# Portioning softmax work between matrix products, and giving the products' PSUM banks a pool of their own, in a two-layer cross-attention kernel

## The chip, the cores and the metric

The kernel runs on one core of one Trainium2 chip. The metric is the time of one execution on the device in microseconds (us), as the median of several runs. The core's engines work side by side and meet by semaphores: PE does the matrix products and transposes and writes its results into PSUM, which has eight banks; DVE (vectors), ACT (activations, copies) empty them; POOL does some elementwise work and issues the stores; SP issues the loads.

## The reference

Two layers of cross-attention over the same context, for B = 8 batch items of S = 100 tokens with C = 640 channels and 20 heads of 32. The context has 722 rows of 1024: the first 77 are text, the other 645 are image rows.

```python
# layer 0
q = split(x @ Wq.T);  k, v = split(text @ Wk.T), split(text @ Wv.T)
k_ip, v_ip = split(ip @ Wk_ip.T), split(ip @ Wv_ip.T)
out = attend(q, k, v) + attend(q, k_ip, v_ip)          # softmax(q k / sqrt(32)) v, each
x = out @ Wo.T + bo + x
# layer 1: the same with weights not transposed, and
text_probs = softmax(q_all @ k_text_all.T / sqrt(32))  # over all 640 channels
sem = (text_probs @ text) @ ip.T / sqrt(32)
ip_probs = softmax(scores_ip + 0.5 * sem) * spatial_mask
x = (text_out + ip_probs @ v_ip) @ Wout + bout + x
```

All of it is in fp32. Text and image have a softmax each.

## The kernel before

**Prologue.** Inside a `with` block the queries of layer 0 and the keys and values of the text rows of both layers are made and stored to device memory. Products of two blocks by two blocks are done with seven block products in place of eight (`seven`, lines 158 to 205): first, sixth, second, seventh, fifth, fourth, third. The second and the third add to the bank that the first and the fifth have opened; before they may, ACT has copied the first out (L172), and DVE has combined the fifth with another block (L192). The others are emptied by ACT (L181) or DVE (L177 to L203). The functions of the prologue are `text_k`, `text_v`, `text_v_blocks`, `left_v`, `left_text`, and `sums_of`, which makes the weights' sums (L131 to L134). Every product takes its bank from `product_ps`, which asks the pool `pj[0]`; in the prologue that is `ps_first`, with all eight banks. After the block the pools `ps_sc` (one tile of four banks for scores), `ps_pt` (two banks, for transposes and small products) and `ps_pj` (two banks, for products) take their place.

**Main loop.** A unit u is one batch item of one layer (16 in all), and in it p runs over five groups of four heads; n = 5u + p counts the 80 steps. In a step the kernel does the attention of group (u, p) and, in between, produces keys and values of the image rows for later units. Production is a list of tasks, each one product or a part of one of about 2 us, with a due time in steps (`spread`, from rough costs). `make(until)` runs the tasks whose due time has come; `between` puts them around small products (output projection `out_piece`, next queries `q_piece`, and the four functions `sem_...` for layer 1). The tasks are those of `pair_tasks` (two batch items at a time with `seven`: psv and psk; `last_k` makes the fifth block of keys, L503, copied by ACT at L509), then `single_tasks` and `last_tasks` (plain products, L608, copied at L610).

The order in a step is: scores part 0 (512 image rows); products; transposes 0 and 1 of the step before; products; transposes 2 and 3; scores part 1 (133 image rows and 77 text rows); products; transposes 4 and 5; products; `values` of the step before (pv, L927). After each pair of transposes, DVE (L912) or ACT (L910, blocks 2 and 5) copies the transposed block out.

`scores` (line 840) multiplies queries with keys into the tile sc (L849) and then asks for the whole softmax of that part at once: the negated maxima (one DVE reduce over four heads for layer 0, L855; for layer 1 one DVE operation a head, L862, that also adds sem), an exponential a head (ACT, L866), and for part 1 the text maxima (L872), the text exponentials (L874), the factors that join the two parts (L879 to L887), and the scaling of the probabilities p (four ACT operations L889, two DVE operations L890 and L893).

**What sets the order.** The loop is in a `manual_schedule` for PE: PE runs exactly in the order of the code. The instructions of the other engines are put in order by the framework ahead of the run, and on the chip each engine follows that fixed order.

Of the kernel before, what the change touches and what calls it, by code (L numbers as in the profile page):

```python
# [10 lines left out]
AF = mybir.ActivationFunctionType  # L11
ALU = mybir.AluOpType
AX = mybir.AxisListType
# [3 lines left out]
S = 100  # L17
C = 640
CC = 1024
NT = 77  # L20
NI = 645
NL = NI - 5 * P
NK = NI + NT
KA = 512
KB = NK - KA
# [18 lines left out]
def two_layer_xattn(  # L44
# [17 lines left out]
    nc = tc.nc  # L62
    PSUM = bass.MemoryType.PSUM
# [22 lines left out]
    mask_sb = const.tile([S, 2], F32, tag="mask", name="mask_sb")  # L86
# [52 lines left out]
    def load_wk(src):  # L139
        load_quarters("k", src, 2 * P)  # L140
        W["k", 4] = wpool.tile([P, NCC, P], F32, tag="wk4", name="wk4")
        nc.sync.dma_start(W["k", 4], src.rearrange("(k p) n -> p k n", p=P)[:, :, 4 * P :])
# [7 lines left out]

    def product_ps(name):
        return pj[0].tile([P, 512], F32, tag="pj", name=name)

    pj = []

    def seven(name, product, area, beside=None):

# [59 lines left out]
    TR = TH - 2 * P  # L219
    with ExitStack() as es:  # L220
        fp = es.enter_context(tc.tile_pool(name="first", bufs=1))
        pj.append(es.enter_context(tc.tile_pool(name="ps_first", bufs=8, space=PSUM)))
        xt = fp.tile([P, B, NC_, S], F32, tag="x", name="xt")
        wq0 = []
        nc.sync.dma_start(xt[:, :2], x_t[:, :2])
# [6 lines left out]
        text = fp.tile([P, NCC, B * NT], F32, tag="text", name="text")  # L232
# [12 lines left out]
        for g in range(B // 2):  # L245
# [10 lines left out]
            for i in range(3):  # L256
                n = 2 if i < 2 else 1
# [7 lines left out]
        st = fp.tile([P, 4, HK, TH], F32, tag="s", name="s_text")  # L265
# [53 lines left out]
                    t[64 * h : 64 * h + TR, :, :HC],  # L319
                )  # L320

        def text_v_blocks(l, rows=(0, 1)):
            for r in rows:
                t = fp.tile([P, 2, 2, HC], F32, tag="evs", name=f"vt_{l}_{r}", bufs=2)

                def product(ps, which, go_on, r=r):
                    for k in range(HK):
                        nc.tensor.matmul(
                            ps[:, :HC], lhsT=sums[which][:, k, r * P : (r + 1) * P], rhs=W["v", WHICH[which]][:, k, :],
                            start=(k == 0 and not go_on), stop=(k == HK - 1), skip_group_check=True,  # L330
                        )

                for f in seven(f"psvt_{l}_{r}", product, tuple(t[:, h, m] for h in range(2) for m in range(2))):
                    f()
                for h in range(2):
                    nc.gpsimd.dma_start(
                        vt_d[l][h * TH + r * P : h * TH + (r + 1) * P, :].rearrange("r (m n) -> r m n", m=2), t[:, h]
                    )
# [3 lines left out]
        def load_left(l):  # L342
            for k in range(NCC):
                wl[l, k] = fp.tile([P, C], F32, tag="wr", name=f"wl_{l}_{k}", bufs=NCC)
                nc.sync.dma_start(wl[l, k], wvi[l][k * P : (k + 1) * P, :])
# [37 lines left out]
        def sums_of(kind):  # L383
            weight_sums(kind, {"v": HC, "k": 2 * P}[kind], (nc.vector, nc.gpsimd))

        with tc.manual_schedule(engines={mybir.EngineType.PE}):
            sums_of("k")
            text_k(0)
            load_wk(wkt[1])
            text_v(0)  # L390
            sums_of("v")
            load_left(0)
            text_v_blocks(0)
            load_wv(wvt[1])
            sums_of("k")
            text_k(1)
            load_wk(wki[0])
            left_v(0)
            load_left(1)
            left_text()  # L400
            text_v(1)
            sums_of("v")
            text_v_blocks(1, (0,))
            sums_of("k")
            left_v(1)
            text_v_blocks(1, (1,))

    ps_sc = ctx.enter_context(tc.tile_pool(name="ps_sc", bufs=1, space=PSUM))
    ps_pt = ctx.enter_context(tc.tile_pool(name="ps_pt", bufs=2, space=PSUM))
    pj[0] = ctx.enter_context(tc.tile_pool(name="ps_pj", bufs=2, space=PSUM))  # L410
    opool = ctx.enter_context(tc.tile_pool(name="made", bufs=2))
    kpool = ctx.enter_context(tc.tile_pool(name="k", bufs=2))
    vpool = ctx.enter_context(tc.tile_pool(name="v", bufs=2))
# [5 lines left out]
    ks, vs, qs_, vts, sems, texts, kt5 = {}, {}, {}, {}, {}, {}, {}  # L419
# [417 lines left out]

    pr, stats, sct = {}, {}, {}

    def scores(u, c, part):  # L840
        k0, k1 = ((0, KA), (KA, NK))[part]
        if part == 0:
            pr[u, c] = ppool.tile([S, 4, NK], F32, tag="p", name=f"p_{u}_{c}")

            stats[u, c] = stat.tile([S, 14, 4], F32, tag="st", name=f"st_{u}_{c}")
        sc = ps_sc.tile([P, 4, 512], F32, tag="sc", name=f"sc_{u}_{c}_{part}")
        for i in range(4):
            rows = slice(32 * i, 32 * i + 32)
            nc.tensor.matmul(  # L849
                sc[:S, i, : k1 - k0], lhsT=qs_[u][rows, c, :], rhs=ks[u, c][rows, k0:k1], start=True, stop=True  # L850
            )
        p, st, l = pr[u, c], stats[u, c], u // B
        n = min(k1, NI) - k0
        if l == 0:
            nc.vector.tensor_reduce(st[:, part, :], sc[:S, :, :n], AX.X, ALU.max, negate=True)  # L855
        for i in range(4):
            if l == 0:
                img, sign = sc[:S, i, :n], 1.0
            else:

                img, sign = p[:, i, k0 : k0 + n], -1.0
                nc.vector.tensor_tensor_reduce(  # L862
                    out=img, in0=sc[:S, i, :n], in1=sems[u][:, k0 : k0 + n], scale=-1.0, scalar=3.0e38,
                    op0=ALU.add, op1=ALU.min, accum_out=st[:, part, i : i + 1],
                )
            nc.scalar.activation(  # L866
                p[:, i, k0 : k0 + n], img, AF.Exp, bias=st[:, part, i : i + 1], scale=sign,
                accum_out=st[:, 3 + part, i : i + 1],
            )
        if part == 0:  # L870
            return
        nc.vector.tensor_reduce(st[:, 2, :], sc[:S, :, n:KB], AX.X, ALU.max, negate=True)  # L872
        for i in range(4):
            nc.scalar.activation(  # L874
                p[:, i, NI:], sc[:S, i, n:KB], AF.Exp, bias=st[:, 2, i : i + 1], accum_out=st[:, 5, i : i + 1]
            )

        lo, f, rz, mul = st[:, 6, :], st[:, 7:9, :], st[:, 9:11, :], st[:, 11:13, :]
        nc.vector.tensor_tensor(lo, st[:, 0, :], st[:, 1, :], ALU.min)  # L879
        nc.vector.tensor_tensor(f, lo.unsqueeze(1).to_broadcast([S, 2, 4]), st[:, 0:2, :], ALU.subtract)  # L880
        nc.scalar.activation(f, f, AF.Exp)
        nc.vector.tensor_tensor(st[:, 3:5, :], st[:, 3:5, :], f, ALU.mult)
        nc.vector.tensor_tensor(st[:, 4, :], st[:, 3, :], st[:, 4, :], ALU.add)
        nc.vector.reciprocal(rz, st[:, 4:6, :])
        nc.vector.scalar_tensor_tensor(  # L885
            mul, f, mask_sb[:, l : l + 1], rz[:, 0:1, :].to_broadcast([S, 2, 4]), ALU.mult, ALU.mult
        )  # L887
        for i in range(4):
            nc.scalar.activation(p[:, i, :KA], p[:, i, :KA], AF.Copy, scale=mul[:, 0, i : i + 1])  # L889
        nc.vector.tensor_tensor(  # L890
            p[:, :, KA:NI], p[:, :, KA:NI], mul[:, 1, :].unsqueeze(2).to_broadcast([S, 4, NI - KA]), ALU.mult
        )
        nc.vector.tensor_tensor(  # L893
            p[:, :, NI:], p[:, :, NI:], rz[:, 1, :].unsqueeze(2).to_broadcast([S, 4, NT]), ALU.mult
        )

    pts = {}

    def transposes(u, c, j):
        if j == 0:  # L900
            pts[u, c] = one.tile([P, 6, 4 * S], F32, tag="pt", name=f"pt_{u}_{c}")
        rows = P if j < 5 else NTAIL
        ps = ps_pt.tile([P, 512], F32, tag="pt", name=f"pspt_{u}_{c}_{j}")
        for i in range(4):
            nc.tensor.transpose(  # L905
                ps[:rows, i * S : (i + 1) * S], pr[u, c][:, i, j * P : j * P + rows], ident[:S, :S]
            )
        dst, src = pts[u, c][:rows, j, :], ps[:rows, : 4 * S]
        if j % 3 == 2:
            nc.scalar.copy(dst, src)  # L910
        else:
            nc.vector.tensor_copy(dst, src)  # L912
# [126 lines left out]
    with tc.manual_schedule(engines={mybir.EngineType.PE}):  # L1039
# [5 lines left out]
        todo = production()  # L1045
        done = [0]

        def make(until):
            while done[0] < len(todo) and todo[done[0]][1] < until:
                todo[done[0]][2]()  # L1050
                done[0] += 1

        mark = [0]

        def apart(until):

            while done[0] < len(todo) and todo[done[0]][1] < until and not any(
                t for t, _, _ in todo[mark[0] : done[0]]
            ):
                todo[done[0]][2]()  # L1060
                done[0] += 1
            mark[0] = done[0]

        def between(n, a, b, small):
# [11 lines left out]
        for u in range(NU):  # L1076
            for p in range(NC_):
                n = NC_ * u + p
# [78 lines left out]
```

## Time and profile before

| what | value |
|---|---|
| median of 3 runs | 2101.18 us (2100.68 to 2103.62) |
| the profiled execution's own time | 2102.57 us |
| its span, first to last instruction | 2100.8 us |
| granted clock of PE | 1.000 |
| prologue, up to the first product of the loop | 207.6 us |
| first scores | 396 us |

The span is 1.8 us shorter than the execution's own time. Rows of groups read: line, engine, operation, output <- input, shapes, count | busy us, mean ns of one | idle time of the engine just before them, and what ended it. In the timeline a row begins with its start and its duration; a bracket gives the idle time of its engine just before it and what released it.

### The profile page before, as it was taken

The page shows a single profiled execution, that of the slowest core. Times are in us where ns is not written, and L with a number is a line of the kernel's source. Part 1 is how long each engine was busy: PE and PEld are TensorE (multiplying, and loading weights), DVE is VectorE, ACT ScalarE, POOL GpSimd, SP SyncE. Part 2 cuts the span into 40 slices and gives each one's busy share as a digit, 9 for nine tenths or more (in the row PEclk, how much of TensorE's full clock was granted, in tenths as well). Part 3 has the DMA queues.
Part 4 walks back from the last instruction along what each step waited for, and adds up shares of the span by engine and source line. Part 5 has one row for each costly group of instructions (what it writes and reads, how often), then busy time and mean ns, then how long its engine had stood idle before and what let it go on. Part 6 is the DMA issues. An engine that isn't in the chain of part 4 may idle for free.

```text
span 2100.8 us, 40948 instructions
## 1 busy us (share of the span) xinstructions
PE 2069.5 (99%) x16370; PEld 1635.0 (78%) x16370; DVE 941.5 (45%) x2420; ACT 863.6 (41%) x2865; POOL 332.6 (16%) x378
## 2 busy tenths in 40 slices
PE   8999999999999999999999999999999999999999
PEld 8676787777787777787788877887878778777888
DVE  1211221345544554444454545445455454555554
ACT  1001000244433544344444544445444455676665
POOL 3313221111111111111150110111111110101110
PEclk9999999999999999999999999999999999999999
DMA  9344232323424443352544443353344345434320
GB/s 343 113 133 152 91 95 77 113 74 87 111 80 131 124 113 92 95 160 80 153 130 127 131 106 81 112 146 97 82 116 132 94 122 153 141 101 118 112 83 7
DMA packets 272493, 241.96 MB, mean 115 GB/s; under 512 B 42798, under 2 KB 241890, under 8 KB 272302
## 3 DMA queue, kind: packets, MB, share of 16 engines
q1 hardware_dynamic: 253182, 171.97, 30.0%
q0 software_dynamic: 19120, 67.37, 9.7%
q8 instruction: 129, 2.11, 0.4%
q14 instruction: 62, 0.51, 0.1%
HBM read 171.68 MB, written 67.61 MB: 114 GB/s over the span
## 4 chain that ended last, share of the span: by engine, by line
PE 95%; DVE 2%; ACT 1%; DMA 1%; issue 1%; SPq 0%; DVEq 0%; ACTq 0%
PE psv_a L528 8%; PE psv_d L528 8%; PE pspt L905 8%; PE psk_d L536 6%; PE sc L849 6%; PE psk_a L536 6%; PE psk L503 5%; PE pv L927 4%; PE psv L608 4%; PE psv_e L528 4%; PE psk L608 4%; PE psv_c L528 4%; PE psv_b L528 3%; PE psk_b L536 3%; PE psk_e L536 3%; PE psk_c L536 3%
## 5 line engine op out<-in xcount | busy, mean ns | idle before, releaser
L912 DVE COPY pt<-pspt 128x400 f32<-128x400 f32 x320 | 176.2, 569 | 191.3 <-PE pspt L905 184.2
L866 ACT ACTIVATE p<-p,st 100x512 f32<-100x512 f32 (+1 forms) x320 | 176.4, 553 | 134.6 <-DVE st L862 134.5
L866 ACT ACTIVATE p<-sc,st 100x512 f32<-100x512 f32 (+1 forms) x320 | 165.0, 528 | 142.7 <-DVE st L855 142.5
L905 PE MATMUL pspt<-ident,p 100*128 100x100 f32 (+1 forms) x1920 | 212.6, 250 | 10.3 <-DVE res L779 4.9
L905 PEld LDWEIGHTS pspt<-ident,p 100*128 100x128 f32 (+1 forms) x1920 | 187.7, 138 | 44.0 <-DVE res L779 8.5
L889 ACT ACTIVATE p<-p,st 100x512 f32<-100x512 f32 x320 | 204.8, 711 | 37.9 <-DVE st L885 37.5
L528 PE MATMUL psv_a<-wv,x 128*128 128x397 f32 (+1 forms) x560 | 185.5, 473 | 2.6 <-ACT vo L172 2.6
L910 ACT COPY pt<-pspt 128x400 f32<-128x400 f32 (+1 forms) x160 | 78.1, 488 | 253.9 <-PE pspt L905 253.1
L528 PE MATMUL psv_d<-wv,s 128*128 128x320 f32 (+1 forms) x560 | 174.7, 455 | 0.0
L528 PEld LDWEIGHTS psv_a<-wv,x 128*128 128x128 f32 x560 | 103.2, 190 | 67.1 <-issue 9.4
L552 POOL DMA_DIRECT2D v_d<-vo x70 | 39.5, 564 | 725.1 <-DVE gst L520 389.8
L862 DVE CUSTOM_DVE_ANT_0 p<-sc,sem 100x512 f32<-100x512 f32 (+1 forms) x320 | 138.8, 490 | 28.5 <-PE sc L849 28.5
L528 PEld LDWEIGHTS psv_d<-wv,s 128*128 128x128 f32 x560 | 103.9, 190 | 55.7 <-issue 5.8
L536 PEld LDWEIGHTS psk_a<-x,wk 128*128 128x128 f32 x1120 | 132.3, 192 | 12.8 <-issue 9.4
L536 PE MATMUL psk_d<-s,wk 128*128 128x128 f32 (+1 forms) x1120 | 140.0, 278 | 0.4 <-ACT ko L181 0.4
L536 PE MATMUL psk_a<-x,wk 128*128 128x128 f32 (+1 forms) x1120 | 139.2, 277 | 0.0
L849 PE MATMUL sc<-k,q 32*100 32x210 f32 (+1 forms) x1280 | 138.6, 502 | 0.3 <-ACT p L874 0.3
L536 PEld LDWEIGHTS psk_d<-s,wk 128*128 128x128 f32 x1120 | 131.2, 192 | 9.1 <-issue 3.3
L855 DVE TENSOR_REDUCE st<-sc 100x4 f32<-100x2048 f32 x80 | 120.1, 1501 | 30.4 <-PE sc L849 30.3
L503 PE MATMUL psk<-x,wk 128*128 128x256 f32 (+1 forms) x560 | 131.6, 383 | 0.7 <-DVE vt L203 0.7
L564 POOL DMA_DIRECT2D k_d<-ko x70 | 58.1, 829 | 463.2 <-DVE ko L198 427.2
L503 PEld LDWEIGHTS psk<-x,wk 128*128 128x128 f32 x560 | 102.3, 189 | 23.6 <-issue 8.5
(180 smaller groups left out, 3302.3 us busy)
## 6 DMA issues: line engine op xcount, KB each, us to landing
x<-ip_t SPq DMA_DIRECT2D x56, 512.0 KB
k<-k_d SPq DMA_DIRECT2D x78, 322.5 KB
v<-v_d SPq DMA_DIRECT2D x78, 320.0 KB
v_d<-vo POOLq DMA_DIRECT2D x70, 320.0 KB, 2.6
k_d<-ko POOLq DMA_DIRECT2D x56, 320.0 KB, 6.9
o<-wo SPq DMA_DIRECT2D x40, 320.0 KB
x<-ip_t SPq DMA_DIRECT2D x16, 532.0 KB
q<-wq SPq DMA_DIRECT2D x20, 320.0 KB
```

The costliest lines, as they stand in the source:

```text
L503: nc.tensor.matmul(ps[:, : 2 * n], lhsT=W["k", 4][:, k, :], rhs=xs[j][:, :, k, :n], start=(k == 0), stop=(k == NCC - 1),)
L528: nc.tensor.matmul(ps[:, :m], lhsT=sums[which][:, k, :P], rhs=w[:, k, :], start=(k == 0 and not go_on), stop=(k == HK - 1), skip_group_che ...
L536: nc.tensor.matmul(ps[:, r * n : (r + 1) * n], lhsT=W["k", WHICH[which]][:, k, r * P : (r + 1) * P], rhs=sums[which][:, k, :], start=(r == ...
L608: nc.tensor.matmul(ps[:m, :n], lhsT=lhs(k), rhs=rhs(k), start=(k == 0), stop=(k == NCC - 1))
L849: nc.tensor.matmul(sc[:S, i, : k1 - k0], lhsT=qs_[u][rows, c, :], rhs=ks[u, c][rows, k0:k1], start=True, stop=True)
L855: nc.vector.tensor_reduce(st[:, part, :], sc[:S, :, :n], AX.X, ALU.max, negate=True)
L862: nc.vector.tensor_tensor_reduce(out=img, in0=sc[:S, i, :n], in1=sems[u][:, k0 : k0 + n], scale=-1.0, scalar=3.0e38, op0=ALU.add, op1=ALU. ...
L866: nc.scalar.activation(p[:, i, k0 : k0 + n], img, AF.Exp, bias=st[:, part, i : i + 1], scale=sign, accum_out=st[:, 3 + part, i : i + 1],)
L889: nc.scalar.activation(p[:, i, :KA], p[:, i, :KA], AF.Copy, scale=mul[:, 0, i : i + 1])
L905: nc.tensor.transpose(ps[:rows, i * S : (i + 1) * S], pr[u, c][:, i, j * P : j * P + rows], ident[:S, :S])
L912: nc.vector.tensor_copy(dst, src)
L927: nc.tensor.matmul(ps[32 * i : 32 * i + 32, :S], lhsT=lhs, rhs=pt[:rows, j, i * S : (i + 1) * S], start=(j == 0), stop=(j == 5),)
```

## The change

1. `ps_pj` (two banks) is opened ahead of the prologue and used by the loop alone; `ps_first` has six banks in place of eight.
2. At the end of the prologue `text_v_blocks(1)` runs its two halves together, and `left_v(1)` comes last; before, `left_v(1)` stood between the halves.
3. `scores` asks at once only for the first maxima. The rest goes into a list `later` as portions. For part 0: the exponentials of heads 0 and 1 with the maxima of heads 2 and 3; the exponentials of heads 2 and 3. For part 1: the four exponentials with the text maxima; the text exponentials with the sums; the factors with the scaling of heads 0 and 1 and of the image rest; the scaling of heads 2 and 3 and of the text. The reduce of part 0 in layer 0 becomes two, over two heads each.
4. After every task that has a cost, `next_task` asks for one portion. `scores` first asks for all portions that read the banks of sc (`free_scores`), and transposes 0 ask for all that is left.

```diff
+    ps_pj = ctx.enter_context(tc.tile_pool(name="ps_pj", bufs=2, space=PSUM))
+    pj = []
...
-        pj.append(es.enter_context(tc.tile_pool(name="ps_first", bufs=8, space=PSUM)))
+        pj.append(es.enter_context(tc.tile_pool(name="ps_first", bufs=6, space=PSUM)))
...
-            text_v_blocks(1, (0,))
+            text_v_blocks(1)
             sums_of("k")
             left_v(1)
-            text_v_blocks(1, (1,))
...
-    pj[0] = ctx.enter_context(tc.tile_pool(name="ps_pj", bufs=2, space=PSUM))
+    pj[0] = ps_pj
...
+    later = []
+    def emit(n):
+        for _ in range(n):
+            later.pop(0)[1]()
+    def free_scores():
+        emit(max([i + 1 for i, (r, _) in enumerate(later) if r], default=0))
...
     def scores(u, c, part):
         k0, k1 = ((0, KA), (KA, NK))[part]
+        free_scores()
...
         if part == 0:
-            return
...
+            maxima((0, 1))
+            later.append((True, lambda: (exponentials((0, 1)), maxima((2, 3)))))
+            later.append((True, lambda: exponentials((2, 3))))
+        else:
+            maxima((0, 1, 2, 3))
+            later.append((True, lambda: (exponentials((0, 1, 2, 3)), text_maxima())))
+            later.append((True, text_exponentials))
+            later.append((False, lambda: (factors(), scaled((0, 1)), scaled_rest(False))))
+            later.append((False, lambda: (scaled((2, 3)), scaled_rest(True))))
...
     def transposes(u, c, j):
         if j == 0:
+            emit(len(later))
...
+        def next_task():
+            todo[done[0]][2]()
+            if todo[done[0]][0] and later:
+                emit(1)
+            done[0] += 1
+
         def make(until):
             while done[0] < len(todo) and todo[done[0]][1] < until:
-                todo[done[0]][2]()
-                done[0] += 1
+                next_task()
```

`maxima`, `exponentials`, `text_maxima`, `text_exponentials`, `factors`, `scaled` and `scaled_rest` are the old statements of `scores`, cut into functions that take the heads. `apart`, which puts a product between two small ones, calls `next_task` in the same way.

More of the change, by code (lines that the diff above doesn't have):

```diff
@@ L149, in load_x @@
         return t
+    ps_pj = ctx.enter_context(tc.tile_pool(name="ps_pj", bufs=2, space=PSUM))
+    pj = []
     def product_ps(name):
         return pj[0].tile([P, 512], F32, tag="pj", name=name)
-    pj = []
     def seven(name, product, area, beside=None):
@@ L320, in text_v, with text_v_blocks @@
                 )
-        def text_v_blocks(l, rows=(0, 1)):
-            for r in rows:
+        def text_v_blocks(l):
+            for r in range(2):
                 t = fp.tile([P, 2, 2, HC], F32, tag="evs", name=f"vt_{l}_{r}", bufs=2)
@@ L853, in scores, with maxima @@
         n = min(k1, NI) - k0
-        if l == 0:
-            nc.vector.tensor_reduce(st[:, part, :], sc[:S, :, :n], AX.X, ALU.max, negate=True)
-        for i in range(4):
+        lo, f, rz, mul = st[:, 6, :], st[:, 7:9, :], st[:, 9:11, :], st[:, 11:13, :]
+        def maxima(heads):
             if l == 0:
-                img, sign = sc[:S, i, :n], 1.0
-            else:
[L861 to L864, printed above, removed]
-                )
[L866 to L869, printed above, removed]
+                nc.vector.tensor_reduce(
+                    st[:, part, heads[0] : heads[-1] + 1], sc[:S, heads[0] : heads[-1] + 1, :n], AX.X, ALU.max,
+                    negate=True,
+                )
+                return
+            for i in heads:
+                nc.vector.tensor_tensor_reduce(
+                    out=p[:, i, k0 : k0 + n], in0=sc[:S, i, :n], in1=sems[u][:, k0 : k0 + n], scale=-1.0,
+                    scalar=3.0e38, op0=ALU.add, op1=ALU.min, accum_out=st[:, part, i : i + 1],
+                )
@@ new lines, in exponentials, with text_maxima @@
+        def exponentials(heads):
+            for i in heads:
+                dst = p[:, i, k0 : k0 + n]
+                nc.scalar.activation(
+                    dst, dst if l else sc[:S, i, :n], AF.Exp, bias=st[:, part, i : i + 1],
+                    scale=-1.0 if l else 1.0, accum_out=st[:, 3 + part, i : i + 1],
+                )
+        def text_maxima():
+            nc.vector.tensor_reduce(st[:, 2, :], sc[:S, :, n:KB], AX.X, ALU.max, negate=True)
+            nc.vector.tensor_tensor(lo, st[:, 0, :], st[:, 1, :], ALU.min)
+            nc.vector.tensor_tensor(f, lo.unsqueeze(1).to_broadcast([S, 2, 4]), st[:, 0:2, :], ALU.subtract)
@@ new lines, in text_exponentials, with factors @@
+        def text_exponentials():
+            nc.scalar.activation(f, f, AF.Exp)
+            for i in range(4):
+                nc.scalar.activation(
+                    p[:, i, NI:], sc[:S, i, n:KB], AF.Exp, bias=st[:, 2, i : i + 1], accum_out=st[:, 5, i : i + 1]
+                )
+            nc.vector.tensor_tensor(st[:, 3:5, :], st[:, 3:5, :], f, ALU.mult)
+            nc.vector.tensor_tensor(st[:, 4, :], st[:, 3, :], st[:, 4, :], ALU.add)
+        def factors():
+            nc.vector.reciprocal(rz, st[:, 4:6, :])
+            nc.vector.scalar_tensor_tensor(
+                mul, f, mask_sb[:, l : l + 1], rz[:, 0:1, :].to_broadcast([S, 2, 4]), ALU.mult, ALU.mult
+            )
@@ new lines, in scaled, with scaled_rest @@
+        def scaled(heads):
+            for i in heads:
+                nc.scalar.activation(p[:, i, :KA], p[:, i, :KA], AF.Copy, scale=mul[:, 0, i : i + 1])
+        def scaled_rest(text):
+            if text:
+                nc.vector.tensor_tensor(
+                    p[:, :, NI:], p[:, :, NI:], rz[:, 1, :].unsqueeze(2).to_broadcast([S, 4, NT]), ALU.mult
+                )
+            else:
+                nc.vector.tensor_tensor(
+                    p[:, :, KA:NI], p[:, :, KA:NI], mul[:, 1, :].unsqueeze(2).to_broadcast([S, 4, NI - KA]),
+                    ALU.mult,
+                )
@@ L870, in scores @@
         if part == 0:
-            return
[L872 to L895, printed above, removed]
+            maxima((0, 1))
[7 more added lines that the diff above has]
+            later.append((False, lambda: (scaled((2, 3)), scaled_rest(True))))
@@ L1059, in apart @@
             ):
-                todo[done[0]][2]()
-                done[0] += 1
+                next_task()
             mark[0] = done[0]
```

## The prediction

> **What bounds the kernel now.** I read the page first: busy time by engine, then the chain that ended last.
>
> ```profile
> span 2100.8 us, 40948 instructions
> PE 2069.5 (99%) x16370; PEld 1635.0 (78%) x16370; DVE 941.5 (45%) x2420; ACT 863.6 (41%) x2865; POOL 332.6 (16%) x378
> PE 95%; DVE 2%; ACT 1%; DMA 1%; issue 1%; SPq 0%; DVEq 0%; ACTq 0%
> ```
>
> PE is busy for 2069.5 of 2100.8 us, and the chain runs 95% through it. DVE and ACT stand at 45% and 41%. The diff touches no shape of a matmul, so it can win or lose only in PE's 31.3 us of idle time, about 5 us of which lie at the start before the first weights land. What fills the rest is in the view of waits, for PE alone (line, tile, waited for: us in total, times, longest):
>
> ```profile
> PE pspt L905 <- DVE res L779: 4.9, 15, 1.3
> PE pspt L905 <- DVE pt L912: 4.3, 7, 0.7
> PE pv L927 <- DVE pt L912: 3.3, 6, 1.1
> PE psv_a L528 <- ACT vo L172: 2.6, 4, 1.0
> PE psk_b L536 <- ACT ko L509: 1.7, 1, 1.7
> PE pv L927 <- ACT pt L910: 0.7, 2, 0.4
> PE psk L503 <- DVE vt L203: 0.7, 1, 0.7
> PE psk_d L536 <- ACT ko L181: 0.4, 1, 0.4
> PE sc L849 <- ACT p L874: 0.3, 1, 0.3
> ```
>
> Nearly every wait is for DVE or ACT to empty a PSUM bank or to copy a transposed block. I went to the instants in the timeline. The first is typical of softmax work standing ahead of an eviction:
>
> ```profile
> 1294.33 0.47 DVE L893 TENSOR_TENSOR p<-p,st 100x308 f32<-100x308 f32 x1
> 1294.50 2.56 ACT L889 ACTIVATE p<-p,st 100x512 f32<-100x512 f32 x4 [1.93 <-DVE st L885]
> 1294.71 0.70 DVE L890 TENSOR_TENSOR p<-p,st 100x532 f32<-100x532 f32 x1
> 1295.51 0.56 DVE L912 COPY pt<-pspt 128x400 f32<-128x400 f32 x1
> 1296.12 1.07 PE L927 MATMUL pv<-pt,v 128*32 128x100 f32 x40 [1.01 <-DVE pt L912]
> 1296.96 0.47 ACT L910 COPY pt<-pspt 82x400 f32<-82x400 f32 x1
> ```
>
> The transposes ended near 1293.4. Their DVE copy (L912) started at 1295.51, behind the two scalings L893 and L890; ACT's copy (L910) came only after its four scalings (L889). PE waits for both. Layer 0 has the same with its exponentials (the window cuts the last line at six of eight):
>
> ```profile
> 420.82 0.69 ACT L866 ACTIVATE p<-sc,st 100x512 f32<-100x512 f32 x1
> 421.48 0.43 ACT L172 COPY vo<-psv_a 128x320 f32<-128x320 f32 x1
> 421.97 2.27 PE L528 MATMUL psv_a<-wv,x 128*128 128x397 f32 x6 [1.01 <-ACT vo L172]
> ```
>
> And where the prologue meets the loop:
>
> ```profile
> 212.88 1.49 DVE L131 TENSOR_TENSOR wvt<-wv,wv 128x1280 f32<-128x1280 f32 x1 [5.42 <-DMA wv<-wvi]
> 214.38 0.37 ACT L509 COPY ko<-psk 128x256 f32<-128x256 f32 x1 [15.60 <-DVE wvt L131]
> 214.81 2.05 PE L536 MATMUL psk_b<-s,wkt 128*128 128x128 f32 x16 [1.72 <-ACT ko L509]
> ```
>
> The product psk was done at 211.1; its copy ran at 214.38, released by a weight sum that itself waited for a weight load, and psk_b needed the bank.
>
> [...] with two banks the products mostly run without a gap, and the gaps appear when an evacuation is late.
>
> **The change, part by part.**
>
> *Priority.* Only PE's order is written by hand. On DVE and ACT the order of the code acts as a priority, not as a sequence: in the timeline the copy L910 at 1574.26 ran ahead of the four scalings L889 (1576.77) that `scores` had asked for earlier, and L131 at 212.88 ran before evictions that the code asks for earlier. So a portion asked for later does not have to run later; it loses only when a copy of a product is ready too. I expect exponentials, text exponentials and scalings to stand at nearly their old times, with evictions ahead of them where they meet.
> - ACT: psv_a 2.6 and psk_d 0.4 waited behind exponentials, pv 0.7 behind scalings: 3.7 us.
> - DVE: of pv's 3.3, two of 1.06 us are behind scalings: 2.1. Of the 4.9 for L779, two of 1.29 have scalings in front; the other thirteen average (4.9 - 2.6) / 13 = 0.18 us, which is the plain evacuation of an output piece with two banks, and stays. So 2 x (1.29 - 0.18) = 2.2. Together 4.3 us.
> - The 4.3 for L912 are about 0.67 each late in the run, where two transposes follow each other closely beside the semantic logits; I count nothing, at best half (2 us).
>
> *Smaller maxima.* For layer 0 the 40 reduces of 100x2048 (2292 ns each in the groups by form) become 80 of 100x1024. From 2292 and the 711 ns of 100x532: slope 1581 / 1516 = 1.04 ns a column, 0.16 us fixed. So one is about 1.22 us, and DVE has 40 x 0.16 = 6.4 us more. [...] With DVE at 45% this lies beside PE: no cost on the path. An eviction behind a reduce now waits at most 1.2 us in place of 2.3. No exponential, scaling or copy is added or removed.
>
> *PSUM.* The loop's two product banks exist from the start, and the prologue keeps six of eight. The prologue's longest need is one `seven`, which runs on two banks later without a gap; the query products take three banks per pair, so six hold two pairs, and a pair's copy has a whole pair's PE time (9.3 us). Cost nothing. The wait of psk for L203 (0.7 us) goes.
>
> *Order at the prologue's end.* text_v_blocks(1) runs whole before left_v(1). Its second half (56 instructions, seven evictions, two DMA issues of 0.55 us on POOL) moves 4.4 us forward; left_v (32 instructions, two ACT copies of 0.43, two issues on POOL, 1.06 in all) becomes last. SP's loads of wv waited for that half to finish reading (issue at 206.97), so they too start 4.4 us sooner, and L131 ends near 210 in place of 214.4. psk_b needs its bank at about 212. The 1.7 us go; cover is thin by some 2 us, so from 0 to 1.7. left_v's copies and two DMAs (issue 1.06 us, and 2.6 us to landing for the same queue's writes) end within 5 us of left_v, inside last_k plus psk_a (5.6 us). The weights' sum for k was made at 161.8 to 170, so nothing there is late. Sum 2.4 us.
>
> *What is late next.* Readers of the scores' four banks now have lower priority, so the next scores can wait: 0.3 us in the whole run today. At 1559 to 1580 the last reader of part 0 ends 4.8 us ahead of part 1, that of part 1 6.1 us ahead of the next part 0. The code lets the first portion follow one product and the second two, about 2.2 us each. Bound: 0 if priority alone acts; if portions really follow the products, 4.4 us and the four text exponentials (1.3 us from the first to the last in the timeline) meet a slack of 6.1. I take 0.04 us for each of 80: 3.2 us. The scaled probabilities are needed only by transposes, 10 us and more later; nothing.
>
> Sum: 3.7 + 4.3 + 2.4 - 3.2 = 7.2 us saved. The profiled execution took 2102.57 us (1.8 us outside its span): 2102.57 - 7.2 = 2095.4. The median of the runs is 2101.18, 1.4 lower: **2094.0 us**.
>
> **Rivals.**
> *No difference that shows* (0.2%, 4.2 us, is about what a measurement of this kernel can tell). Two forms: waits only change places, because the order of DVE and ACT is fixed ahead and meets other durations on the chip; or only the prologue's meeting point is won, 2101.2 - 2.4 = 2098.8. For it: of the 31.3 us of idle time, 31.3 - 10.4 = 20.9 are reached by no step of mine. Chance 0.26.
>
> *Softmax becomes late, slower.* Place: the scores' banks between part 1 and the next part 0, freed by the text exponentials, and where few products lie between them (from 1800 us on, ACT 67%). For it: one product copy that is late on the chip holds the exponentials queued behind it. Against: ACT's and DVE's idle halves. It decides when a scores group waits over 10.4 / 80 = 0.13 us on average; slower by 0.2% from 0.18. With 0.4 us on half of 80, and a like amount on part 1: 32 - 10.4 = 21 us, 2122; with half of that, 2107. Chance 0.25.
>
> *Better than the sum*: the 0.67 us waits shrink and nothing is late: 2101.2 - 10.4 - 2 = 2088.8; inside the faster case.
>
> **How the numbers follow.** Forecast (faster) 0.49, no difference 0.26, slower 0.25. The forecast's own range is 2086 to 2097. All the idle time in reach could give no more than some 15 us (2086), which is the low end. Above, half of the slower case is kept, up to 2110.
>
> **What would show it.** Right: PE's waits for L172's, L910's and L912's successors lose their entries near 1 us; psk_b and psk at 207 to 215 us run without a gap; PE's idle falls to about 24 us; waits for L779 stay near 0.18 each. Wrong: waits of sc for the exponentials in tens of entries, or a PE wait of pspt for the scaling, or an early gap in the prologue for a bank. DVE's busy time should rise by some 6 us.

## The result and the profile after

| | median | range | runs |
|---|---|---|---|
| before | 2101.90 us | 2100.68 to 2103.93 | 6 |
| changed | 2087.29 us | 2086.36 to 2089.78 | 6 |

The ratio is 0.9931, 95% interval 0.9918 to 0.9943. That is 0.0069 x 2101.9 = 14.5 us faster, inside the range that was given, in the direction of the forecast, and twice the 7.2 us of its sum.

The page of the changed kernel, the lines that answer to those of before:

```profile
span 2085.4 us, 40990 instructions
PE 2065.0 (99%) x16370; PEld 1630.3 (78%) x16370; DVE 948.3 (45%) x2460; ACT 869.3 (42%) x2865; POOL 333.6 (16%) x378
PE 96%; ACT 1%; DVE 1%; issue 0%; DMA 0%; SPq 0%; DVEq 0%; ACTq 0%
```

The same 16370 matmuls; the 40 new reduces are in DVE's count, and DVE's busy time is up by 6.8 us, near the 6.4 of the step on maxima. PE is still the bound (99% busy, 96% of the chain). The span fell by 15.4 us. Of that, PE's idle time gave 31.3 - 20.4 = 10.9 and PE's busy time 2069.5 - 2065.0 = 4.5, with not one matmul less. Of these 4.5, 0.9 are no gain of the change: they lie in the first query products (37.1 us busy before, 36.2 after), and that busy time ranges from 35.8 to 37.1 us over all the runs, in kernels with and without the change.

The view of waits, PE alone (waited for: us in total, times, longest). Line numbers of the prologue and of the products moved by up to one, those of `scores` and behind it by 11 to 40: L945 are the transposes, L952 and L950 their copies on DVE and ACT, L967 is pv, L860 sc, L884 the exponentials, L898 the text exponentials, L912 the scalings on ACT.

```profile
PE pspt L945 <- DVE res L779: 2.8, 15, 0.3
PE pv L967 <- DVE pt L952: 1.7, 5, 0.6
PE pspt L945 <- ACT tp L727: 1.3, 3, 0.4
PE pspt L945 <- ACT sem L757: 0.8, 3, 0.4
PE sc L860 <- ACT p L884: 0.6, 1, 0.6
PE pspt L945 <- DVE pt L952: 0.3, 1, 0.3
PE sc L860 <- ACT p L898: 0.3, 1, 0.3
```

The entries near 1 us are gone: psv_a for ACT's copy (4 times), psk_b, psk and psk_d have no wait left, pv none for ACT. The 15 waits for L779 are still 15, but the longest is 0.3 where it was 1.3: 2.8 / 15 = 0.19 on average. The six of 0.67 for the copy of a transposed block have become six of about 0.35 for the semantic logits' own work (L727, L757). And the scores wait 0.9 us in all, where they waited 0.3.

The place in layer 0 that the prediction showed. Before, with what led up to it (PEld is PE's weight load):

```profile
415.66 2.56 ACT L889 ACTIVATE p<-p,st 100x512 f32<-100x512 f32 x4 [1.05 <-DVE st L885]
418.13 0.35 ACT L509 COPY ko<-psk 128x256 f32<-128x256 f32 x1
418.53 1.91 PEld L528 LDWEIGHTS psv_b<-wvt,s 128*128 128x128 f32 x8 [0.52 <-ACT ko L509]
418.53 2.42 PE L528 MATMUL psv_b<-wvt,s 128*128 128x320 f32 x8
```

In the timeline after:

```profile
412.91 0.35 ACT L509 COPY ko<-psk 128x256 f32<-128x256 f32 x1
413.16 1.95 ACT L912 ACTIVATE p<-p,st 100x512 f32<-100x512 f32 x3
413.17 1.22 DVE L869 TENSOR_REDUCE st<-sc 100x2 f32<-100x1024 f32 x1
414.26 2.14 PEld L528 LDWEIGHTS psv_b<-wvt,s 128*128 128x128 f32 x8
414.60 2.31 PE L528 MATMUL psv_b<-wvt,s 128*128 128x320 f32 x8
415.67 0.68 ACT L884 ACTIVATE p<-sc,st 100x512 f32<-100x512 f32 x1
416.33 0.42 ACT L173 COPY vo<-psv_a 128x320 f32<-128x320 f32 x1
416.47 1.23 DVE L869 TENSOR_REDUCE st<-sc 100x2 f32<-100x1024 f32 x1 [2.08 <-ACT p L884]
416.81 2.94 PE L528 MATMUL psv_a<-wv,x 128*128 128x397 f32 x8
```

ACT's copy (L173) now stands behind two exponentials and not four, and psv_a starts without a bracket. From the start of psv_b to that of psv_a it is 2.21 us. Before it was 421.97 - 418.53 = 3.44 us, with a wait of 1.01 shown. So 1.23 us are gone at this place and the view of PE's waits had shown 1.01. Half of the other 0.22 belongs to another late copy: psv_b's weight load had waited 0.52 us for L509, which stood behind the four scalings, and so it began together with its matmuls, which then took 2.42 us and not 2.31. The rest is overlap: psv_a now starts at 416.81, 0.10 us before the listed end of psv_b (414.60 + 2.31).

The meeting of prologue and loop:

```profile
205.68 3.72 PE L503 MATMUL psk<-x,wk 128*128 128x256 f32 x16
206.55 1.49 DVE L131 TENSOR_TENSOR wvt<-wv,wv 128x1280 f32<-128x1280 f32 x1 [4.71 <-DMA wv<-wvi]
209.24 1.94 PE L536 MATMUL psk_a<-x,wk 128*128 128x128 f32 x16
209.57 0.37 ACT L509 COPY ko<-psk 128x256 f32<-128x256 f32 x1 [2.92 <-PE psk L503]
211.02 1.95 PE L536 MATMUL psk_b<-s,wkt 128*128 128x128 f32 x16
```

L131 starts at 206.55, 6.3 us sooner than before, and the copy of psk waits for its product alone. psk itself starts at 205.68 without a wait, on a bank of its own.

### The profile page after: what moved, and what is told of

It is laid out like the page before. It is cut to its first block, busy times and chain, and to the rows that moved or that the text cites. A ratio compares the mean times of both kernels' runs of the same rounds, so it can differ in the third digit from the quotient of the medians.

```text
span 2085.4 us, 40990 instructions
## 1 busy us (share of the span) xinstructions
PE 2065.0 (99%) x16370; PEld 1630.3 (78%) x16370; DVE 948.3 (45%) x2460; ACT 869.3 (42%) x2865; POOL 333.6 (16%) x378
## 4 chain that ended last, share of the span: by engine, by line
PE 96%; ACT 1%; DVE 1%; issue 0%; DMA 0%; SPq 0%; DVEq 0%; ACTq 0%
PE psv_a L528 8%; PE psv_d L528 8%; PE pspt L945 7%; PE psk_d L536 6%; PE psk_a L536 6%; PE sc L860 6%; PE psk L503 6%; PE pv L967 5%; PE psv_e L528 4%; PE psv L608 4%; PE psk L608 4%; PE psv_b L528 4%; PE psv_c L528 4%; PE psk_b L536 3%; PE psk_e L536 3%; PE psk_c L536 3%
## 5 line engine op out<-in xcount | busy, mean ns | idle before, releaser
L884 ACT ACTIVATE p<-sc,st 100x512 f32<-100x512 f32 (+1 forms) x320 | 166.3, 528 | 225.2 <-DVE st L869 225.1
L952 DVE COPY pt<-pspt 128x400 f32<-128x400 f32 x320 | 176.2, 570 | 170.5 <-PE pspt L945 166.7
L884 ACT ACTIVATE p<-p,st 100x512 f32<-100x512 f32 (+1 forms) x320 | 177.0, 555 | 131.7 <-DVE st L876 131.4
L912 ACT ACTIVATE p<-p,st 100x512 f32<-100x512 f32 x320 | 210.3, 714 | 45.7 <-DVE st L906 45.3
L945 PEld LDWEIGHTS pspt<-ident,p 100*128 100x128 f32 (+1 forms) x1920 | 187.4, 137 | 39.6 <-DVE res L779 6.4
L945 PE MATMUL pspt<-ident,p 100*128 100x100 f32 (+1 forms) x1920 | 211.9, 250 | 6.2 <-DVE res L779 2.8
L950 ACT COPY pt<-pspt 128x400 f32<-128x400 f32 (+1 forms) x160 | 77.9, 487 | 244.2 <-PE pspt L945 243.3
L869 DVE TENSOR_REDUCE st<-sc 100x2 f32<-100x1024 f32 (+1 forms) x120 | 126.2, 1052 | 68.1 <-ACT p L884 37.7
L860 PE MATMUL sc<-k,q 32*100 32x210 f32 (+1 forms) x1280 | 138.5, 502 | 1.1 <-ACT p L884 0.6
```

The lines of the kernel that those rows point to most:

```text
L860: nc.tensor.matmul(sc[:S, i, : k1 - k0], lhsT=qs_[u][rows, c, :], rhs=ks[u, c][rows, k0:k1], start=True, stop=True)
L869: nc.vector.tensor_reduce(st[:, part, heads[0] : heads[-1] + 1], sc[:S, heads[0] : heads[-1] + 1, :n], AX.X, ALU.max, negate=True,)
L884: nc.scalar.activation(dst, dst if l else sc[:S, i, :n], AF.Exp, bias=st[:, part, i : i + 1], scale=-1.0 if l else 1.0, accum_out=st[:, 3 ...
L945: nc.tensor.transpose(ps[:rows, i * S : (i + 1) * S], pr[u, c][:, i, j * P : j * P + rows], ident[:S, :S])
```

## The experiments

Theory A: on DVE and ACT the order of asking is a priority; evictions go ahead of softmax work that is asked for later, and softmax work has time. Its rivals are named in the expectations. Each ratio is against the kernel before, in runs on the same chip.

**The portions alone, and the prologue alone.** The change was cut in two. The first half is the changed kernel with its new `scores`, but with the old banks and the old order of the prologue (diff against the changed kernel; `text_v_blocks` takes the halves as an argument again).

```diff
-    ps_pj = ctx.enter_context(tc.tile_pool(name="ps_pj", bufs=2, space=PSUM))
...
-        pj.append(... name="ps_first", bufs=6 ...)
+        pj.append(... name="ps_first", bufs=8 ...)
...
-            text_v_blocks(1)
+            text_v_blocks(1, (0,))
             sums_of("k")
             left_v(1)
+            text_v_blocks(1, (1,))
...
-    pj[0] = ps_pj
+    pj[0] = ctx.enter_context(tc.tile_pool(name="ps_pj", bufs=2, space=PSUM))
```

> The portions alone, with the prologue's order and banks as before. Theory A (evictions ahead of softmax work): the gains in the loop stay, the two gaps at 207 and 215 us (0.7 and 1.7 us listed) come back, so about 2.7 us short of the full change: 11 to 12 us faster than before, 2090. Rival B (most of the gain is the earlier start of the loop, which also shifts what collides later): under 6 us faster, above 2095.

Measured 2089.47 us, ratio 0.9940 (0.9927 to 0.9952): 12.6 us faster. The two gaps are back in the view of waits, psk_b with 1.9 and psk with 0.7 us.

The other half is the kernel before with only the two banks and the new order of the prologue.

```diff
+    ps_pj = ctx.enter_context(tc.tile_pool(name="ps_pj", bufs=2, space=PSUM))
...
-        pj.append(... name="ps_first", bufs=8 ...)
+        pj.append(... name="ps_first", bufs=6 ...)
...
-            text_v_blocks(1, (0,))
+            text_v_blocks(1)
             sums_of("k")
             left_v(1)
-            text_v_blocks(1, (1,))
...
-    pj[0] = ctx.enter_context(tc.tile_pool(name="ps_pj", bufs=2, space=PSUM))
+    pj[0] = ps_pj
```

> The product banks of their own and the prologue's order alone, scores as before. Theory A: the gaps at 207 and 215 us go, 2.5 to 4 us faster than before, 2098 to 2099.5; the listed waits for L172, L779 and L912 near 1 us stay. Rival B: 8 us or more faster.

Measured 2098.60 us, ratio 0.9980 (0.9973 to 0.9988): 4.2 us faster, by the medians 3.6. The listed waits of the loop stand as before, psv_a 2.6, pv 3.3, pspt for L779 4.9. The halves add up, 12.6 + 4.2 = 16.8 against 14.5, within their intervals. Rival B falls.

**Order without banks.** The kernel before with only `left_v(1)` moved to the end.

```diff
-            text_v_blocks(1, (0,))
+            text_v_blocks(1)
             sums_of("k")
             left_v(1)
-            text_v_blocks(1, (1,))
```

> Only the order at the prologue's end (left_v last), with eight banks in the prologue and the product banks opened after it. My step: the weight loads start 4.4 us sooner and L131 no longer holds the copy L509, so the 1.7 us gap before psk_b goes, but psk must still wait for the last eviction of the prologue (now ACT's copy of left_v), 0.7 us or more: 1 to 2 us faster than before. Rival: the 1.7 us gap is due to the banks and stays: no difference or slower.

Measured 2099.96 us, ratio 0.9989 (0.9983 to 0.9996), 2.3 us faster. Its waits hold one line of the meeting point:

```profile
PE psk L502 <- ACT vl L360: 1.0, 1, 1.0
```

psk_b's wait is gone with the old banks, so the order removes it, and L131 starts at 207.43 here (212.88 before), after earlier weight loads; psk still waits 1.0 us for the last eviction of the prologue, and that is what banks of its own remove: the run with the prologue alone has no such wait.

**No later asking.** The full change, but every portion is asked for at the end of `scores`.

```diff
             later.append((False, lambda: (scaled((2, 3)), scaled_rest(True))))
+        emit(len(later))
```

> The full change, but scores asks for all its portions at its own end, so nothing is asked for later; the regrouping (maxima of all heads ahead of the exponentials, two reduces in place of one) stays. Theory A (it is the later asking that lets evictions go first): only the prologue's part is left, 2.5 to 5 us faster than before, 2097 to 2099.5. Rival C (the regrouping and the smaller reduces do it): 11 us or more faster, as with the full change.

Measured 2096.49 us, ratio 0.9973 (0.9962 to 0.9983), 5.7 us faster. So most of the loop's gain needs the later asking. But not all: the psv_a waits were gone here too, while pv's wait for ACT's copy rose from 0.7 to 1.7 us.

```profile
PE pspt L946 <- DVE pt L953: 4.3, 7, 0.7
PE pspt L946 <- DVE res L779: 4.1, 15, 0.9
PE pv L968 <- DVE pt L953: 3.0, 6, 1.0
PE pv L968 <- ACT pt L951: 1.7, 5, 0.5
```

**What freed psv_a: the smaller reduces, or the order?** Two runs. In the first, the full change with one whole reduce:

```diff
-            maxima((0, 1))
-            later.append((True, lambda: (exponentials((0, 1)), maxima((2, 3)))))
+            maxima((0, 1, 2, 3))
+            later.append((True, lambda: exponentials((0, 1))))
             later.append((True, lambda: exponentials((2, 3))))
```

> The full change with one reduce of 100x2048 in place of two of 100x1024 in layer 0, the exponentials still in two later portions. The run without delay lost the four psv_a waits (2.6 us listed), so either the smaller reduces or the regrouping did that. Theory E (either is enough: with later exponentials ACT's copy L173 goes first anyway): within 1 us of the full change. Rival F (the smaller reduces alone do it): the psv_a waits come back, 2 to 4 us above the full change.

Measured 2085.76 us, ratio 0.9924 (0.9911 to 0.9938); that interval overlaps the full change's. No psv_a wait came back: rival F falls. DVE's busy time is 941.3 us again, and the scores' wait for L884 (0.6 us) is gone.

In the second, the kernel before with its reduce cut in two and nothing else:

```diff
-            nc.vector.tensor_reduce(st[:, part, :], sc[:S, :, :n], AX.X, ALU.max, negate=True)
+            for h in ((0, 2), (2, 4)) if part == 0 else ((0, 4),):
+                nc.vector.tensor_reduce(
+                    st[:, part, h[0] : h[1]], sc[:S, h[0] : h[1], :n], AX.X, ALU.max, negate=True
+                )
```

> The kernel before with one edit: in layer 0 the reduce of part 0 is two reduces over two heads each, asked for at once, ahead of the exponentials. In the runs with portions or with regrouping the second reduce waits for the exponentials of heads 0 and 1, which leaves ACT's copy L172 a gap to stand in. Here the exponentials can start about 1.07 us sooner (2.29 less 1.22), and L172 still stands behind four of them. Theory H (the length of the first reduce is what made L172 late): three of the four psv_a waits go and the fourth shrinks, 2 to 3 us faster than before. Theory I (the order on ACT is what matters, exponentials start together after both reduces): the psv_a waits stay at 2.6 us listed or grow, no difference from before.

Measured 2101.60 us, ratio 1.0001 (0.9993 to 1.0010): no difference. The psv_a waits are 3.1 us listed. The timeline:

```profile
415.08 2.34 DVE L856 TENSOR_REDUCE st<-sc 100x2 f32<-100x1024 f32 x2
417.52 0.69 ACT L869 ACTIVATE p<-sc,st 100x512 f32<-100x512 f32 x1 [0.47 <-DVE st L856]
419.52 0.69 ACT L869 ACTIVATE p<-sc,st 100x512 f32<-100x512 f32 x1
420.19 0.44 ACT L172 COPY vo<-psv_a 128x320 f32<-128x320 f32 x1
420.68 2.94 PE L528 MATMUL psv_a<-wv,x 128*128 128x397 f32 x8 [1.15 <-ACT vo L172]
```

The exponentials start only after both reduces (415.08 + 2.34 = 417.42), and the copy again stands behind four of them. Theory I holds: the place of L172 in ACT's order is the cause, not the length of the reduce.

**Late scaling alone.** The full change with exponentials asked for at once (`free_scores()` at the end of `scores`); tasks then ask for the two scaling portions only.

```diff
             later.append((False, lambda: (scaled((2, 3)), scaled_rest(True))))
+        free_scores()
```

> The full change, but only the two scaling portions are asked for later; maxima and exponentials are asked for at once in the new grouping (scores ask for every portion that reads their banks at their own end). Theory A: the waits behind scalings (pv for L952, pspt for L779 near 1 us, pv for ACT's copy) go as in the full change, and the psv_a waits are gone as in the run without delay; what comes back are the waits beside the semantic logits that text exponentials delay (2 us). 1 to 3 us above the full change: 2088 to 2090. Rival D (the exponentials' delay carries the gain): 5 us or more above it, 2092 or more.

Measured 2094.84 us, ratio 0.9968 (0.9956 to 0.9981). I had expected 2088 to 2090; rival D's number came. But the timeline shows the scalings still in front of the copies:

```profile
1288.85 2.56 ACT L912 ACTIVATE p<-p,st 100x512 f32<-100x512 f32 x4 [1.86 <-DVE st L906]
1289.53 0.47 DVE L916 TENSOR_TENSOR p<-p,st 100x308 f32<-100x308 f32 x1
1289.92 0.56 DVE L953 COPY pt<-pspt 128x400 f32<-128x400 f32 x1
1290.54 1.07 PE L968 MATMUL pv<-pt,v 128*32 128x100 f32 x40 [1.01 <-DVE pt L953]
```

Without the exponentials ahead of them in the list, the scaling portions were asked for by the first two tasks, which precede transposes 4 and 5. They were later, but not late enough. In the next run no task asks (diff against the run with late scaling). The code then asks for the scaling at the end of the next scores part 0, where `free_scores` empties the list; the expectation says transposes 0, which come a little later. Either way it is after transposes 4 and 5 and `values`.

```diff
-            if todo[done[0]][0] and later:
-                emit(1)
```

> As the run with late scaling alone, but no task asks for a portion: the scaling portions are asked for only at transposes 0 of the next step, that is after transposes 4 and 5 and values. There the scaling portions were first in the list, so the first two tasks after scores part 1 asked for them, still ahead of transposes 4 and 5. Theory A' (a portion helps only when it is asked for after the copy that it stood in front of): the waits of pv for L953 and of pspt for L779 near 1 us go now, 2 to 4 us faster than that run, 2090 to 2093; what the text exponentials delay beside the logits (7 waits of pspt for L953, 4.3 us listed) stays. Rival D (it is the exponentials that must be late): no difference, 2094 to 2096.

Measured 2092.89 us, ratio 0.9956 (0.9944 to 0.9969), some 2 us faster than the run with late scaling by the medians; the intervals overlap, so the trace decides.

```profile
1287.61 0.72 ACT L912 ACTIVATE p<-p,st 100x512 f32<-100x512 f32 x1 [1.87 <-DVE st L906]
1287.67 0.56 DVE L953 COPY pt<-pspt 128x400 f32<-128x400 f32 x1
1288.15 0.70 DVE L920 TENSOR_TENSOR p<-p,st 100x532 f32<-100x532 f32 x1
1288.24 0.47 ACT L951 COPY pt<-pspt 82x400 f32<-82x400 f32 x1
1288.29 1.07 PE L968 MATMUL pv<-pt,v 128*32 128x100 f32 x40
```

Here DVE's copy went ahead of both its scalings, ACT's stood behind one of four, and pv started without a wait. The longest wait for L779 is 0.3 (0.9 in the run with late scaling), pv's for ACT's copy is gone. So Theory A' holds at these places, but not at every one. Of the two waits of pv near 1 us one is left:

```profile
1519.45 0.85 PE L946 MATMUL pspt<-ident,p 100*128 100x100 f32 x8
1521.32 0.47 DVE L916 TENSOR_TENSOR p<-p,st 100x308 f32<-100x308 f32 x1
1521.71 0.70 DVE L920 TENSOR_TENSOR p<-p,st 100x532 f32<-100x532 f32 x1
1522.33 0.56 DVE L953 COPY pt<-pspt 128x400 f32<-128x400 f32 x1
1522.95 1.07 PE L968 MATMUL pv<-pt,v 128*32 128x100 f32 x40 [0.89 <-DVE pt L953]
```

The transposes were done at 1520.30 and the scalings were asked for after the copy, yet both ran ahead of it. In the changed kernel the same place has one scaling ahead and a wait of 0.55. At this place the order of asking did not decide, and pv waited 0.89 us; what decided was not tried.

The 4.3 us for L953 beside the logits stayed, and so did psk_d's 0.4, so these need later exponentials. The full change (ratio 0.9931) is also 0.0025 x 2102 = 5.3 us faster than this run, with intervals that don't overlap. What still differs is mainly that the exponentials come later, so they carry about as much as rival D gave them (5 us or more), and the later scaling some 2 us. The view of PE's waits accounts for half of the 5.3: 1.9 beside the logits, 0.4 at psk_d, 0.3 at pv.

**Half the pace.** The full change, a portion after every second task.

```diff
             if todo[done[0]][0] and later:
-                emit(1)
+                turn[0] += 1
+                if turn[0] % 2 == 0:
+                    emit(1)
```

> The full change, but a portion is asked for only after every second task, so softmax work has a still lower priority and most of it is asked for at the next scores or at transposes 0. Theory A (order of asking is only a priority; what is ready runs): within 1.5 us of the full change, waits of sc under 2 us in all. Rival G (portions follow the products): scores wait for exponentials in tens of entries, 10 us or more slower than the full change.

Measured 2086.72 us, ratio 0.9932 (0.9919 to 0.9944), the same as the full change; the scores wait 0.9 us in all, as there. Rival G, and with it the slower case of the prediction, falls: work that was asked for later still did not reach the next scores later.

**A faster version.** The 15 waits for L779 are left where an output piece stands directly ahead of transposes. The look-ahead for a product to stand between was widened.

```diff
-                apart(n + b + 0.4)
+                apart(n + b + 0.7)
...
-            apart(n + b + 0.4)
+            apart(n + b + 0.7)
```

> The full change, and the look-ahead with which a product is put between two small products is 0.7 step in place of 0.4. Output pieces that stand directly ahead of transposes fall from 19 to 11, next-query pieces from 8 to 2. The waits of pspt for L779 (15 entries, 2.8 us listed) fall by about half: 1 to 2.5 us faster than the full change, 2085 to 2086. Rival: tasks done earlier meet loads or banks that are not ready; the same or slower.

Measured 2084.22 us, ratio 0.9916 (0.9902 to 0.9929). The waits for L779 are 8 of 1.5 us in all. New ones came, one of psv_a with 1.7 us. Together with the whole reduce (both edits are shown above):

> The full change with one whole reduce in layer 0 and the look-ahead of 0.7 step: the two edits that were each 1.5 to 2.5 us faster than the full change. If they add up: 2082 to 2084, below both kernels. Rival: the look-ahead moved the products against the scores, so the wait of sc that the whole reduce removes is no longer there and nothing is added: 2084 to 2085.

Measured 2082.57 us (2082.41 to 2082.76), ratio 0.9909 (0.9895 to 0.9922): 19.1 us faster than before. By the medians the two edits add up (1.5 and 3.1 us below the changed kernel alone, 4.7 together), and the new wait of psv_a is gone. The times lie below every run of the changed kernel, but that ran on another chip, and the intervals of the two ratios still overlap (0.9922 and 0.9918).

## Why the prediction was right, and where its sum was short

- **The bound and the place of the gain.** Right in the main: no matmul changed, and 10.9 of the 15.4 us of span came out of PE's idle time, which fell to 20.4 us (about 24 were expected). But the step said "only" there, and that was wrong by some 3 us (see the last point).
- **Order of asking as a priority.** Right, shown by the run at half the pace (2086.72 us, nothing lost) and by the run with no later asking (2096.49 us, 8 to 9 lost). The step left out a condition: a portion had to be asked for after the copy that it stood in front of, as the two runs with late scaling show (2094.84 and 2092.89 us), and even then one copy came late.
- **ACT, 3.7 us.** The waits went, all seven. As listed they were 2.6 + 0.4 + 0.7. The reason given for psv_a was only half of it: the regrouping without later asking frees it as well.
- **DVE, 4.3 us.** The two waits of 1.29 for L779 went to 0.3 or less (the step left 0.18). pv's wait for L952 fell by 3.3 - 1.7 = 1.6, not 2.1: of the two near 1 us one kept 0.55, behind one scaling.
- **Beside the logits, counted at nothing.** This term was mis-sized. 4.3 us for L912 became 0.3 + 1.3 + 0.8 = 2.4: a gain of 1.9, the "at best half" of the step.
- **What is late next, 3.2 us lost.** Mis-sized most. The scores' waits rose by 0.9 - 0.3 = 0.6 us, in one new entry and not in tens.
- **The prologue, 2.4 us.** Both gaps went, for the reasons given, banks for psk and order for psk_b; alone 4.2 us (2.5 to 5.7 by the interval).
- **The smaller maxima, nothing.** They gave nothing by themselves (ratio 1.0001), and DVE's busy time rose as worked out: one reduce of 100x1024 took 1222 ns on average, where 1.22 us had been estimated from the times of the other two sizes. "No cost on the path" was not quite right: the new wait of the scores, 0.6 us for L884, is there in the changed kernel and gone in the run with one whole reduce.
- **Not in the sum at all.** PE's busy time fell by 4.5 us. Less the 0.9 of the first products, 3.6 are left. In the loop PE has the same matmuls in the same order, so the two traces can be matched one by one: from the start of the first psk to the end of the last matmul they take 13.6 us less (1875.4 against 1889.0). Close to the waits that changed (from 20 matmuls ahead of each to 12 behind it) they take 12.5 us less, and the idle time there fell by 10.5. So about 2 us are cost of these stalls that the view of PE's waits does not list: 0.25 to 0.27 at each of the four psv_a, 0.27 each at psk_b and psk_d, 0.2 at each of two pv. The other 1.6 us are not accounted for.

The terms: 7.2, plus 3.2 - 0.6 = 2.6 for the lateness that did not come, plus 1.9 beside the logits, less 0.5 for pv, plus 4.5 in busy time: 15.7, against 15.4 of the spans. Without the 0.9 that is no gain, 14.8 against the 14.6 of the medians.

So the mechanism was right and the sum was half of what came. The time lies inside the range because its low end was taken from all the idle time in reach; the middle, 2094.0, was 6.7 us too high. What came is the case that the prediction calls better than the sum (2088.8), and the hidden cost of the stalls on top.

## What to carry to other kernels

When one engine is the bound and its order is fixed, look for long runs of low-urgency work that stand ahead of its evictions on the helper engines, and move their place in the order behind the copies that the bound engine waits for; check each move in the timeline, since a move that is not far enough changed little here (5.7 us with no later asking, 6.7 with scaling not late enough). The softmax work had 4.8 and 6.1 us of slack in the step before the change that the prediction read, and 0.6 us of new waits was the price. The share of busy time did not point to any of this: DVE and ACT stood at 45% and 41%. Size a stall from start to start of the waiting engine's instructions, not from the listed wait alone (1.23 us gone against 1.01 listed at psv_a), and look at the weight loads ahead of them too (psv_b's waited 0.52 us for L509).

## What the runs showed that I had not expected

The second reduce of layer 0 waits for the exponentials of the first two heads, though it reads other heads' banks: DVE idles 37.7 us in all before L869 for that (26 times), 2.08 in the instance above. It costs DVE nearly alone; PE has the one wait of 0.6 us for L884, which is missing in the run with one whole reduce. In the kernel with both reduces asked for ahead of the exponentials the opposite holds: the first exponential starts at 417.52, when both reduces are done (417.42). In these two kernels what was asked for later waited for what was asked for earlier; which tile carries the dependency was not tried.
